# Gate and up projections of two token groups by Strassen's seven block products instead of eight

## The chip, the cores and the metric

The kernel runs on one core of one Trainium2 chip. The metric is the device time of one execution in microseconds (us); the time of a kernel is the median of its runs. Its engines are called PE (TensorE, the matrix multiplier), DVE (VectorE), ACT (ScalarE), POOL (GpSimd) and SP (SyncE, which here issues the DMAs). They run beside each other, each through its own instructions in order, and wait for each other by semaphores. PE reads a stationary and a moving matrix from SBUF and adds into PSUM, which has eight banks of 128 x 512 fp32 here.

## The reference

Four blocks follow each other on 2 x 1024 tokens of width 512, each with a layernorm in front and a residual behind; only the last sum is returned:

```python
x = x + attn_a(layernorm(x))   # gated linear attention, 4 heads of 128, chunks of 128 tokens
x = x + ffn(layernorm(x))
x = x + attn_b(layernorm(x))   # softmax attention over 1024 tokens
x = x + ffn(layernorm(x))      # the same weights again

def _qlinear(x, wq, scale):
    W = (wq.astype(float32) - 128.0) * scale[:, None]
    return einsum('bsd,hd->bsh', x, W)
def ffn(x):
    gate = silu(_qlinear(x, wq_gate, s_gate))    # 512 -> 1408
    up = _qlinear(x, wq_up, s_up)                # 512 -> 1408
    return _qlinear(gate * up, wq_down, s_down)  # 1408 -> 512
```

The codes of the FFN weights are integers from 0 to 63, so a weight without its scale is a small integer. All else is fp32.

## The kernel before

*Numbers.* PE multiplies in fp32r, which keeps fewer bits than fp32. `split` (L74) makes two fp32r parts of an fp32 tile: ACT casts (L76), DVE or POOL subtracts (L77). A product of two split matrices takes three matmuls (`mm3`, L93), a product with an FFN weight two, since the integer weight needs no second part.

*Stages.* The 2048 tokens are 16 tiles of 128 (`NT`), or 4 groups of 512 (`NST`). In order: attention a with a prologue that also multiplies the two pairs of weights of attention b together (`weight_product`: M at the start, V in the last two chunks); `ffn` on x1 ("f"); attention b; `ffn` on x3 ("g"). x1, x2 and x3 lie in DRAM between stages.

*Attention a* is a loop over 16 chunks t. In it stand in program order: a head of q for a later group (`q_head`), k and v of the next chunk (`kv_tile`), its decay matrix (`decay`, with a row loaded by SP and masked on POOL, L358), and `scores`, in which k is turned (pkT, L418) and the state updated (pd, L427). `k_norm` of the next chunk is called there: squares on ACT, sums on DVE, a power on POOL (L400), then kb on DVE (L403) and kw on POOL (L410). kb feeds the next pkT, kw the next pd. Layernorms of later groups are spread over the chunks by the list `ln_at`.

*Layernorm of a group* is `ln_step` (L170): four steps, one a tile, on DVE with one power on POOL (L114) and a 32 x 32 transposition on DVE (L178); with the fourth, 16 DMAs on SP's queue (L187) finish the transposition; a fifth step splits the result into xh and xl.

*An FFN* first loads the codes and takes 128 off them on POOL (L91; 22 loads of 128 x 512 for gate and up, 11 for down). Then for each group of 512 tokens: for each of `KH` = 11 blocks j of 128 hidden units, 8 matmuls for gate and 8 for up (L551, L552), Silu on ACT (L555), the product with up on DVE (L558), and its split into hh and hl. When all 11 blocks are done, the four token tiles get their down product, 22 matmuls each (L578, L579), the scale on DVE (L580), the residual on POOL (L582) and the store. The layernorm steps of the next group are called in the j loop; in the last group the steps that the caller gave (`after`).

*Attention b* has, for each batch, q, v, then a loop over 8 query tiles: scores, softmax, transposition of the probabilities through DRAM (stored by L662, loaded as ptl by four DMAs, L670, and split into pth and ptl), and the context pob (L685 calls `mm3`), whose sum x3 is stored. In the second batch the layernorm of g's first group is called in this loop, as the first four and the seventh step.

*Order.* The program is written as above, and a scheduler fixes each engine's order at build time by a model of its own of the times; `issue_after` holds some work behind named instructions. Buffers come from pools with a number of copies: an instruction that writes a new copy waits for the last reader of the oldest. SP issues DMAs in its order, and a DMA that waits holds those behind it.

## Time and profile before

| what | value |
|---|---|
| median of 3 runs | 1009.73 us (1009.11 to 1016.08) |
| profiled execution, its own time | 1013.86 us |
| its span, from the first to the last record | 1012.0 us |
| mean granted PE clock in it | 0.993 of full speed |
| PE busy | 987.8 us, 98% |
| DVE, ACT, POOL busy | 531.3, 294.7, 195.8 us |
| gate and up matmuls (L551, L552) | 4 groups of 352 records, 137.0 to 137.7 us by their durations |
| down matmuls (L578, L579) | 726 records, 275.4 us by their durations |
| code passes on POOL (L91) | 66, 0.65 to 0.76 us each |

The table says how long each engine was busy, not what set the end. A matmul's duration overlaps with the next one's, so that the sum of the durations is larger than the time they took; the steps between starts tell that. In a group of instructions the parts are: line, engine, operation, output <- inputs, shapes and count; after the bar the busy time in us and the mean in ns; after the second bar the idle time of that engine in front of them and whose end it waited for. In a timeline a line begins with the start and the duration in us.

### The profile page before, as it was taken

How to read it: one execution, taken by the hardware profiler on the slowest of the kernel's cores; microseconds unless marked ns; L12 is line 12 of the kernel's file. 1: busy time of each engine (PE TensorE's matmuls, PEld its weight loads, DVE VectorE, ACT ScalarE, POOL GpSimd, SP SyncE). 2: the span in 40 equal slices, each digit the busy share in tenths (PEclk: the TensorE clock that was granted, in tenths of full speed). 3: DMA queues.
4: the chain of work that ended last, by engine and by line, in shares of the span. 5: the costliest groups of instructions: out<-in, count | busy, mean ns of one | idle time of the engine just before them, and what ended most of it. 6: DMA issues, size and time to landing. Idle time of an engine off the chain costs nothing.

```text
span 1012.0 us, 12887 instructions
## 1 busy us (share of the span) xinstructions
PE 987.8 (98%) x4618; PEld 818.6 (81%) x4618; DVE 531.3 (53%) x1075; ACT 294.7 (29%) x554; POOL 195.8 (19%) x242
## 2 busy tenths in 40 slices
PE   9999999988989999999999999999979999999998
PEld 7888888877778888888888887888857888888887
DVE  7577666895574635273634445644536623233232
ACT  5642333331332413232222223222213413122130
POOL 5333222555312020112200000021002020100201
PEclk9999999999999999999999999999998999999999
DMA  8625251479746150454425378477677250110201
GB/s 293 222 86 140 71 118 63 144 189 279 247 111 146 27 136 26 84 206 118 155 42 115 86 165 170 89 177 182 162 146 180 39 125 2 42 42 1 84 1 62
DMA packets 249854, 120.71 MB, mean 119 GB/s; under 512 B 191232, under 2 KB 207936, under 8 KB 249792
## 3 DMA queue, kind: packets, MB, share of 16 engines
q1 hardware_dynamic: 249792, 119.91, 45.6%
q8 instruction: 36, 0.59, 0.2%
q14 instruction: 26, 0.21, 0.1%
HBM read 75.79 MB, written 29.39 MB: 104 GB/s over the span
## 4 chain that ended last, share of the span: by engine, by line
PE 79%; DMA 9%; SPq 5%; DVE 3%; issue 1%; ACT 1%; POOL 1%; ACTq 0%; DVEq 0%; POOLq 0%
PE pgug L551 8%; PE pgug L552 8%; PE pguf L551 6%; PE pguf L552 6%; PE pog L579 4%; PE pog L578 4%; PE pof L579 4%; PE pof L578 4%; DMA ptl<-p 3%; SPq L187 3%; DMA stg_guf<-in_wgu 2%; SPq L670 2%; DMA p<-py 2%; PE pq L96 2%; PE psc L94 1%; PE psc L96 1%
## 5 line engine op out<-in xcount | busy, mean ns | idle before, releaser
L551 PE MATMUL pguf<-xh_f,wguf 128*128 128x512 f32 x352 | 137.5, 391 | 0.3 <-ACT sgf L555 0.3
L551 PE MATMUL pgug<-xh_g,wgug 128*128 128x512 f32 x352 | 137.7, 391 | 0.0
L552 PE MATMUL pgug<-xl_g,wgug 128*128 128x512 f32 x352 | 137.6, 391 | 0.0
L552 PE MATMUL pguf<-xl_f,wguf 128*128 128x512 f32 x352 | 137.0, 389 | 0.0
L551 PEld LDWEIGHTS pguf<-xh_f,wguf 128*128 128x128 f32 x352 | 66.2, 188 | 14.8 <-issue 1.1
L551 PEld LDWEIGHTS pgug<-xh_g,wgug 128*128 128x128 f32 x352 | 66.6, 189 | 13.9
L552 PEld LDWEIGHTS pgug<-xl_g,wgug 128*128 128x128 f32 x352 | 66.5, 189 | 14.0
L552 PEld LDWEIGHTS pguf<-xl_f,wguf 128*128 128x128 f32 x352 | 66.2, 188 | 13.7
L578 PE MATMUL pof<-wdf,hhf 128*128 128x512 f32 x176 | 68.9, 395 | 2.5 <-ACT hhf L76 2.5
L578 PE MATMUL pog<-wdg,hhg 128*128 128x512 f32 (+1 forms) x187 | 68.9, 377 | 0.0
L579 PE MATMUL pog<-wdg,hlg 128*128 128x512 f32 (+1 forms) x187 | 68.8, 377 | 0.0
L579 PE MATMUL pof<-wdf,hlf 128*128 128x512 f32 x176 | 68.8, 395 | 0.0
L558 DVE SCALAR_TENSOR_TENSOR sgg<-pgug,cols,sgg 128x512 f32<-128x512 f32 x44 | 32.9, 748 | 58.0 <-PE pgug L552 58.0
L94 PE MATMUL pob<-vh,pth 128*128 128x512 f32 x128 | 50.7, 396 | 10.6 <-ACT pth L76 10.6
L114 POOL TENSOR_TENSOR rs_g<-ve_g,mhalf 128x1 f32<-128x1 f32 x16 | 8.9, 561 | 247.8 <-DVE ve_g L112 247.8
L582 POOL TENSOR_TENSOR xrg<-og,xrg 128x512 f32<-128x512 f32 x15 | 19.3, 1288 | 187.8 <-DVE og L580 169.6
L76 ACT CAST hhf<-sgf 128x512 fp32r<-128x512 f32 x44 | 27.2, 621 | 84.6 <-DVE sgf L558 76.5
L555 ACT ACTIVATE sgg<-pgug,cols 128x512 f32<-128x512 f32 x44 | 30.3, 688 | 69.7 <-PE pgug L552 60.8
L94 PE MATMUL psc<-xh_b,qh 128*128 128x512 f32 x128 | 50.5, 395 | 0.0
L96 PE MATMUL psc<-xh_b,ql 128*128 128x512 f32 x128 | 50.5, 395 | 0.0
L95 PE MATMUL psc<-xl_b,qh 128*128 128x512 f32 x128 | 50.5, 394 | 0.0
L95 PE MATMUL pob<-vl,pth 128*128 128x512 f32 x128 | 50.1, 391 | 0.0
(222 smaller groups left out, 2091.6 us busy)
## 6 DMA issues: line engine op xcount, KB each, us to landing
p<-py SPq DMA_DIRECT2D x16, 512.0 KB, 3.2
ptl<-p SPq DMA_DIRECT2D x64, 128.0 KB, 3.6
stg_guf<-in_wgu SPq DMA_DIRECT2D x22, 256.0 KB, 4.3
stg_gug<-in_wgu SPq DMA_DIRECT2D x22, 256.0 KB, 3.3
xin_a<-in_x SPq DMA_DIRECT2D x16, 256.0 KB, 4.1
xra<-in_x SPq DMA_DIRECT2D x16, 256.0 KB, 2.9
row<-cl SPq DMA_DIRECT2D x16, 256.0 KB, 3.7
x<-xra SPq DMA_DIRECT2D x16, 256.0 KB, 2.1
```

The lines of the kernel that those rows point to most:

```text
L76: nc.scalar.copy(hi, src)
L94: nc.tensor.matmul(ps, lhs_hi, rhs_hi, start=first, stop=False)
L95: nc.tensor.matmul(ps, lhs_hi, rhs_lo, start=False, stop=False)
L96: nc.tensor.matmul(ps, lhs_lo, rhs_hi, start=False, stop=last)
L187: nc.sync.dma_start(out=xf[32 * b : 32 * (b + 1), :, c, :], in_=y[32 * c : 32 * (c + 1), b].rearrange("p k i q -> p (k i) q"),)
L551: nc.tensor.matmul(ps, w, xh[:, k, :], start=k == 0, stop=False)
L552: nc.tensor.matmul(ps, w, xl[:, k, :], start=False, stop=k == KD - 1)
L555: nc.scalar.activation(sg, pgu[0], AF.Silu, scale=sg_s[:, j : j + 1])
L558: nc.vector.scalar_tensor_tensor(sg, pgu[1], su_s[:, j : j + 1], sg, ALU.mult, ALU.mult)
L578: nc.tensor.matmul(ps, hh[:, cs], wd[j][:, ds], start=j == 0, stop=False)
L579: nc.tensor.matmul(ps, hl[:, cs], wd[j][:, ds], start=False, stop=j == KH - 1)
L670: nc.sync.dma_start(out=raw[32 * r : 32 * (r + 1)].rearrange("p k (c q) -> p (k c) q", c=4), in_=placed[r])
```

## The change

The gate and up weights of one hidden block are a 2 x 2 matrix of blocks (rows gate and up, columns the two halves of the 512 inputs), and the activations of two token groups are another (rows the halves, columns the groups). Their product has eight block products. The change computes it by seven, in Winograd's form of Strassen's method: four sums of weight blocks (s1 to s4), four differences of activations (T1 to T4), and seven sums of results. Each of the products still has two halves of 128 inputs and two fp32r parts of the moving side, 4 matmuls of 512 columns.

- *Weights.* `combine_weights` and `down_weights` are called in chunks 1 to 11 of attention a: codes are loaded, 128 taken off, the four sums made on POOL, and all stored to DRAM. In the FFN, `stationary` loads the seven matrices of a block, 0.92 MB in two DMAs, for each block of each pair of groups, and `wd` is loaded ready made.
- *Activations.* `combine` gives 12 steps: differences in place (on POOL for f's first pair, else DVE), and the split of seven results. f's first pair is combined in chunks 12 to 15, g's in the last tiles of attention b, the second pair of each in the down loop of the first.
- *Results.* In PSUM: X starts with P1, Y with P6, Z with P5, V with P7; ACT copies X and Z, DVE adds; then, one block later (`finish`), P2, P3 and P4 are added by PE on top of what DVE wrote to Z and V.
- *Hidden activations.* They are kept in fp32 (`ha`, `hb`) but for tiles 0 and 1 of the pair, which are split at once (POOL subtracts, DVE for the last block); tiles 2 to 7 are split in the down loop one tile ahead, into two buffers (`hs`).
- *Pools.* The weights, the split activations and the parts share one pool of 12 slots of 128 x 2048.
- *Layernorms.* Those of groups 2 and 3 are in the j loop of the first pair; eight tiles of g are in attention b's second batch in place of four.

```diff
-    wp = ctx.enter_context(tc.tile_pool(name="weights", bufs=12))
-    sp = ctx.enter_context(tc.tile_pool(name="stage", bufs=4))
...
-    tp = ctx.enter_context(tc.tile_pool(name="xT", bufs=3))
...
+    def slot(name, dt=F32R):
+        return wp.tile([P, 2048], dt, tag="slot", name=name)
...
-    def load_codes(dst, src_ap, name):
-
-        stg = sp.tile([P, 512], I32, tag="stg", name=f"stg_{name}")
-        nc.sync.dma_start(out=stg, in_=src_ap)
-        nc.gpsimd.tensor_scalar(dst, stg, -ZERO_POINT, 1.0, ALU.add, ALU.mult)
...
+            raw = lnT[nm, st] = slot(f"xT_{nm}{st}").rearrange("p (k c) -> p k c", k=KD)
...
+            xl = lnT[nm, st]
+            xh = slot(f"xh_{nm}{st}").rearrange("p (k c) -> p k c", k=KD)
             for k in range(KD):
                 split(xh[:, k, :], xl[:, k, :], xl[:, k, :].bitcast(F32))
+            lnT[nm, st] = xh, xl
...
+    def combine(nm, pr, eng):
+        B = {}
+        def begin():
+            ra, rb = (lnT[nm, 2 * pr + n].bitcast(F32) for n in range(2))
+            B.update(B11=ra[:, 0:2], B12=rb[:, 0:2], B21=ra[:, 2:4], B22=rb[:, 2:4])
+        def part(n, src):
+            o = slot(f"{n}_{nm}{pr}").rearrange("p (s k c) -> p s k c", s=2, k=2)
+            XT[nm, pr, n] = o
+            split(o[:, 0], o[:, 1], B[src])
+        def less(dst, x, y):
+            eng.tensor_tensor(B[dst], B[x], B[y], ALU.subtract)
+        return [
+            begin,
+            lambda: part("B11", "B11"),
+            lambda: less("B11", "B12", "B11"),
+            lambda: part("T1", "B11"),
+            lambda: part("B22", "B22"),
+            lambda: less("B12", "B22", "B12"),
+            lambda: less("B22", "B22", "B11"),
+            lambda: part("T2", "B22"),
+            lambda: part("T3", "B12"),
+            lambda: part("B21", "B21"),
+            lambda: less("B21", "B21", "B22"),
+            lambda: part("T4", "B21"),
+        ]
+    def combine_weights(sp, j):
+        g, u = (sp.tile([P, 512], F32, tag="stg", name=f"{n}{j}") for n in ("cg", "cu"))
+        for n, c in enumerate((g, u)):
+            nc.sync.dma_start(out=c.bitcast(I32), in_=a["wgu"][j][:, n * 512 : (n + 1) * 512])
+            nc.gpsimd.tensor_scalar(c, c.bitcast(I32), -ZERO_POINT, 1.0, ALU.add, ALU.mult)
+        s, r = (sp.tile([P, 512], F32, tag="stg", name=f"{n}{j}") for n in ("cs", "cr"))
+        a11, a12, a21, a22 = g[:, 0:256], g[:, 256:512], u[:, 0:256], u[:, 256:512]
+        s1, s2, s3, s4 = s[:, 0:256], s[:, 256:512], r[:, 0:256], r[:, 256:512]
+        nc.gpsimd.tensor_tensor(s1, a21, a22, ALU.add)
+        nc.gpsimd.tensor_tensor(s2, s1, a11, ALU.subtract)
+        nc.gpsimd.tensor_tensor(s3, a11, a21, ALU.subtract)
+        nc.gpsimd.tensor_tensor(s4, a12, s2, ALU.subtract)
+        for n, c in enumerate((g, s, r, u)):
+            nc.sync.dma_start(out=wc_d[j][:, 2 * n : 2 * n + 2], in_=c.rearrange("p (n c) -> p n c", n=2))
+    def down_weights(sp, j):
+        c = sp.tile([P, 512], F32, tag="stg", name=f"cd{j}")
+        nc.sync.dma_start(out=c.bitcast(I32), in_=a["wd"][j])
+        nc.gpsimd.tensor_scalar(c, c.bitcast(I32), -ZERO_POINT, 1.0, ALU.add, ALU.mult)
+        nc.sync.dma_start(out=wd_d[j], in_=c)
+    def stationary(j, name):
+        w = slot(f"wc{name}_{j}").rearrange("p (n c) -> p n c", n=8)
+        nc.sync.dma_start(out=w[:, 0:6].bitcast(F32), in_=wc_d[j][:, 0:6])
+        nc.sync.dma_start(out=w[:, 6:7].bitcast(F32), in_=wc_d[j][:, 7:8])
+        return w
+    def products(ps, w, nm, pr, n, first):
+        m, x = {
+            "P1": (0, "B11"), "P2": (1, "B21"), "P3": (5, "B22"), "P4": (6, "T4"),
+            "P5": (2, "T1"), "P6": (3, "T2"), "P7": (4, "T3"),
+        }[n]
+        o = XT[nm, pr, x]
+        for k in range(2):
+            for s in range(2):
+                nc.tensor.matmul(
+                    ps,
+                    w[:, m, k * P : (k + 1) * P],
+                    o[:, s, k, :],
+                    start=first and k == 0 and s == 0,
+                    stop=k == 1 and s == 1,
+                    skip_group_check=n != "P6",
+                )
...
-            (x1, "f", 0, (8, 9, 10, 11, 14)),
+            (x1, "f", 0, (8, 8, 9, 9)),
+            (x1, "f", 1, (10, 10, 11, 11)),
         ):
             for i, t in enumerate(its):
                 ln_at.setdefault(t, []).append((src, nm, g, i))
+        moving = combine("f", 0, nc.gpsimd)
+        wcs = []
...
+            if 1 <= t <= KH:
+                combine_weights(sp, t - 1)
+                down_weights(sp, t - 1)
+            if t >= NT - 4:
+                for _ in range(3):
+                    moving.pop(0)()
+            if t == NT - 1:
+                wcs += [stationary(j, "f0") for j in range(2)]
...
+            fh = fctx.enter_context(tc.tile_pool(name=f"ffnh{nm}", bufs=1))
+            f1 = fctx.enter_context(tc.tile_pool(name=f"ffn1{nm}", bufs=2))
+            fw = fctx.enter_context(tc.tile_pool(name=f"ffnw{nm}", bufs=KH))
+            fp = fctx.enter_context(tc.tile_pool(name=f"ffn{nm}", bufs=4))
+            wd = []
+            for pr in range(2):
+                if pr == 0:
+                    early = [lambda g=g, i=i: ln_step(src, nm, g, i) for g in (2, 3) for i in range(ST)]
+                    late = combine(nm, 1, nc.vector)
...
+                ha = fh.tile([P, 2, KH, P], F32, tag="ha", name=f"ha{nm}{pr}")
+                hb = fh.tile([P, ST, KH, P], F32, tag="hb", name=f"hb{nm}{pr}")
+                hs = {}
...
+                def h_split(i, js, src, eng):
+                    if i not in hs:
+                        hs[i] = f1.tile([P, 2, KH, P], F32R, tag="hs", name=f"hs{nm}{pr}_{i}")
+                    split(hs[i][:, 0, js], hs[i][:, 1, js], src, eng)
+                def finish(j, w, X, Z, V, up):
+                    products(X, w, nm, pr, "P2", False)
+                    products(Z, w, nm, pr, "P3", False)
+                    products(V, w, nm, pr, "P4", False)
+                    tiles = lambda x: x.rearrange("p (i c) -> p i c", c=P)
+                    su = su_s[:, j : j + 1]
+                    sg = fp.tile([P, 512], F32, tag="sg", name=f"sg{nm}{pr}_{j}")
+                    nc.scalar.activation(sg, X, AF.Silu, scale=sg_s[:, j : j + 1])
+                    nc.scalar.activation(hb[:, :, j], tiles(Z), AF.Silu, scale=sg_s[:, j : j + 1])
+                    h01 = sg[:, 0:256]
+                    nc.vector.scalar_tensor_tensor(h01, V[:, 0:256], su, h01, ALU.mult, ALU.mult)
+                    nc.vector.scalar_tensor_tensor(
+                        ha[:, :, j], tiles(V[:, 256:512]), su, tiles(sg[:, 256:512]), ALU.mult, ALU.mult
+                    )
+                    nc.vector.scalar_tensor_tensor(hb[:, :, j], tiles(up), su, hb[:, :, j], ALU.mult, ALU.mult)
+                    for i in range(2):
+                        h_split(i, j, h01[:, i * P : (i + 1) * P], None if j == KH - 1 else nc.gpsimd)
...
-                    for s in range(2):
-                        ps = psum(f"pgu{nm}{st}_{j}_{s}")
-                        for k in range(KD):
-                            w = wgu[j][:, s * 512 + k * P : s * 512 + (k + 1) * P]
-                            nc.tensor.matmul(ps, w, xh[:, k, :], start=k == 0, stop=False)
-                            nc.tensor.matmul(ps, w, xl[:, k, :], start=False, stop=k == KD - 1)
-                        pgu.append(ps)
-                    sg = fp.tile([P, 512], F32, tag="sg", name=f"sg{nm}{st}_{j}")
-                    nc.scalar.activation(sg, pgu[0], AF.Silu, scale=sg_s[:, j : j + 1])
-                    hh = f1.tile([P, 512], F32R, tag="hh", name=f"hh{nm}{st}_{j}")
-                    hl = f1.tile([P, 512], F32R, tag="hl", name=f"hl{nm}{st}_{j}")
-                    nc.vector.scalar_tensor_tensor(sg, pgu[1], su_s[:, j : j + 1], sg, ALU.mult, ALU.mult)
-                    split(hh, hl, sg)
-                    hT.append((hh, hl))
-                    if steps and (len(steps) > 1 or j == KH - 1):
-                        ln_step(*steps.pop(0))
-                for i in range(ST):
-                    for step in steps:
-                        ln_step(*step)
-                    steps = []
-                    t = st * ST + i
-                    cs = bass.ts(i, P)
+                    for n in range(len(wcs), min(j + 3, KH)):
+                        wcs.append(stationary(n, f"{nm}{pr}"))
+                    w = wcs[j]
+                    X, Y, Z, V = (psum(f"p{n}{nm}{pr}_{j}") for n in "XYZV")
+                    for ps, n in ((X, "P1"), (Y, "P6"), (Z, "P5"), (V, "P7")):
+                        products(ps, w, nm, pr, n, True)
+                    u2 = fp.tile([P, 512], F32, tag="sg", name=f"u2{nm}{pr}_{j}")
+                    nc.scalar.copy(u2, X)
+                    nc.vector.tensor_tensor(u2, Y, u2, ALU.add)
+                    up = fp.tile([P, 512], F32, tag="sg", name=f"up{nm}{pr}_{j}")
+                    nc.scalar.copy(up, Z)
+                    nc.vector.tensor_tensor(Z, Z, u2, ALU.add)
+                    nc.vector.tensor_tensor(V, V, u2, ALU.add)
+                    nc.vector.tensor_tensor(up, V, up, ALU.add)
+                    if begun:
+                        finish(*begun)
+                    begun = j, w, X, Z, V, up
+                    if early:
+                        early.pop(0)()
+                    if pr == 0:
+                        d = fw.tile([P, 512], F32R, tag="wd", name=f"wd{nm}{j}")
+                        nc.sync.dma_start(out=d.bitcast(F32), in_=wd_d[j])
+                        wd.append(d)
...
+                finish(*begun)
+                wcs = []
+                for i in range(2 * ST):
+                    t = pr * 2 * ST + i
+                    if 1 <= i < 2 * ST - 1:
+                        n = i + 1
+                        for js in (slice(0, 6), slice(6, KH)):
+                            h_split(n, js, ha[:, n - 2, js] if n < ST else hb[:, n - ST, js], None)
...
-                            hh, hl = hT[j]
-                            nc.tensor.matmul(ps, hh[:, cs], wd[j][:, ds], start=j == 0, stop=False)
-                            nc.tensor.matmul(ps, hl[:, cs], wd[j][:, ds], start=False, stop=j == KH - 1)
+                            nc.tensor.matmul(ps, hs[i][:, 0, j], wd[j][:, ds], start=j == 0, stop=False)
+                            nc.tensor.matmul(ps, hs[i][:, 1, j], wd[j][:, ds], start=False, stop=j == KH - 1)
...
+                    for _ in range(2):
+                        if late:
+                            late.pop(0)()
+                    if pr == 0 and i == 4:
+                        wcs = [stationary(n, f"{nm}1") for n in range(2)]
+    b_first = [lambda g=g, i=i: ln_step(x2, "b", g, i) for g in range(2) for i in range(ST)]
+    b_split = [lambda g=g: ln_step(x2, "b", g, ST) for g in range(2)]
+    ffn(x1, x2, "f", wcs, (b_first, b_split))
...
-                nxt = (x2, "b", 2 * b + 2) if b + 1 < NB else (x3, "g", 0)
-                if i < 4:
-                    ln_step(*nxt, i)
-                if i == 6:
-                    ln_step(*nxt, 4)
-                    if b + 1 < NB:
+                if b + 1 < NB:
+                    if i < 4:
+                        ln_step(x2, "b", 2 * b + 2, i)
+                    else:
+                        ln_step(x2, "b", 2 * b + 3, i - 4)
+                    if i == 6:
+                        ln_step(x2, "b", 2 * b + 2, 4)
                         xTs[b + 1, 0] = lnT["b", 2 * b + 2]
-                if b + 1 < NB and i >= 4:
-                    ln_step(x2, "b", 2 * b + 3, i - 4)
+                else:
+                    if i < 6:
+                        for n in (0, 1) if i < 2 else (0,):
+                            g = 2 * i + n if i < 2 else i + 2
+                            ln_step(x3, "g", *divmod(g, ST))
+                    else:
+                        for _ in range(5):
+                            moving.pop(0)()
...
+        for _ in range(2):
+            moving.pop(0)()
+        wcs = [stationary(n, "g0") for n in range(2)]
```

## The prediction

> **What bounds the kernel now.** I read the table of engines first, then the chain that ended last, the windows by stage, the list of PE's waits, and the timelines around the places that change.
>
> ```profile
> span 1012.0 us, 12887 instructions
> PE 987.8 (98%) x4618; PEld 818.6 (81%) x4618; DVE 531.3 (53%) x1075; ACT 294.7 (29%) x554; POOL 195.8 (19%) x242
> PE 79%; DMA 9%; SPq 5%; DVE 3%; issue 1%; ACT 1%; POOL 1%; ACTq 0%; DVEq 0%; POOLq 0%
> ```
>
> TensorE is busy for all but 24.2 of 1012.0 us, so removed matmuls are worth their full time, and every new hole in PE costs its full length. What a matmul is worth is its pitch, since their ends overlap:
>
> ```profile
> 399.81 0.39 PE L551 MATMUL pguf<-xh_f,wguf 128*128 128x512 f32 x1
> ...
> 401.63 0.39 PE L551 MATMUL pguf<-xh_f,wguf 128*128 128x512 f32 x1
> ```
>
> Eight steps lie between these starts: 1.82 / 8 = 0.2275 us each, not the 0.39 in the column of durations. The windows (PE, PEld, DVE, ACT, POOL busy; clock; DMA share; GB/s) show where there is room:
>
> ```profile
> 100.00:200.00 100.00, 100.00 (x594) 86.94 (x593) 69.62 (x171) 37.17 (x81) 32.82 (x36) 1.00 0.36 101
> 200.00:225.00 25.00, 21.57 (x138) 18.48 (x137) 23.08 (x51) 8.93 (x20) 13.77 (x17) 1.00 0.70 174
> 225.00:250.00 25.00, 22.40 (x117) 19.45 (x116) 15.91 (x36) 3.96 (x6) 13.45 (x21) 0.93 0.93 269
> 800.00:950.00 150.00, 150.00 (x663) 124.22 (x662) 49.23 (x71) 35.35 (x55) 14.87 (x12) 1.00 0.16 46
> ```
>
> In attention a PE never waits while POOL is a third busy; its end (200 to 250) is where PE idles, 3.4 and 2.6 us; in the FFN (800 to 950) everything but PE is below 35%.
>
> **The change part by part,** against the profiled execution (1013.86 us: the span and 1.86 around it), which is 4.1 above the median of 1009.73.
>
> 1. *Matmuls.* Per hidden block and pair of groups 7 products of 4 replace 8 of 4. There are 11 x 2 x 2 = 44 such blocks: 44 x 4 = 176 fewer, and the built instruction order has 4362 matmul rows before, 4186 after. 176 x 0.2275 = **-40.0**. Everything below is what this pays for.
>
> 2. *Sums of weights in attention a.* Chunks 1 to 11 each get, on POOL, 3 code passes of 128x512 (0.69 by the row of L91) and 4 sums of 128x256. No row has such a sum; bounds: rs of one column, 0.55, and kw of 512, 1.04. I take 0.65, by the code pass of twice the width at 0.69. Per chunk 3 x 0.69 + 4 x 0.65 = 4.7 us; 11 chunks 51 us. On SP 3 loads and 5 stores, 8 issues of 0.33 to 0.4, so 2.9 us a chunk. In a settled chunk the cover is this:
>
> ```profile
> 103.93 1.01 POOL L400 TENSOR_TENSOR s<-ss,mhalf 128x4 f32<-128x4 f32 x1 [0.22 <-DVE ss L398]
> 105.71 0.69 DVE L403 TENSOR_TENSOR kb<-sWk,s 128x512 f32<-128x512 f32 x1
> 106.62 1.04 POOL L410 TENSOR_TENSOR kw<-sWk,s 128x512 f32<-128x512 f32 x1 [1.67 <-DVE s L408]
> 113.35 0.60 PE L418 MATMUL pkT<-ident,kb 128*128 128x128 f32 x4
> ```
>
> kb is done 7 us before its transpose, kw some 6 us before pd. A POOL sum that waits for its codes (a 256 KB code load lands in 4.3) holds s, kw, sdec, rs and the mask (L358) behind it. Load, passes and store by stage slots of four make a round of 4.3 + 4.7 + about 2.5 for a store (x1's lands in 2.1, issue 0.35) = 11.5 us against a chunk of 13, so it keeps up, later. At the start it does not: s(0) is at 41.7 and s(1) at 55.3, and two rounds stand between them in program order: 41.7 + 1.0 + 2 x 11.5 = 66, kb(1) at 67, wanted by pkT(1) at 62.2. That is 5 us of stall, 2 more for kw: 7, and 1 for later slips: **+8**, bounds 0 (the scheduler finds room) to 22 (two more such slips).
>
> 3. *End of attention a.* Four differences 128x1024 on POOL (twice kw's 1.04 to L582's 1.29: 2.1 to 2.6 each, some 10 in all) and the four casts and subtractions of 1024 on DVE (py's 1.24) come among the last chunks; the chain of code loads and passes that made the 3.4 and 2.6 us holes goes. Late next are kb(15) behind DVE's 1024-wide work (5 us) and the V product. **0**, bounds -6 to +8.
>
> 4. *The gate/up loop.* A block is 28 x 0.2275 = 6.4 us. DVE gets 4 combining passes and 3 products (four and one of 512 at 0.60 pitch, two of 256 at 0.43): 3.9; ACT two copies, two Silu, two casts of 128 : 0.6 + 0.6 + 1.4 + 0.8 = 3.4. Both are below 6.4. Two of the additions write PSUM in place, which no row shows; between the price of a row that reads PSUM (0.68) and double it, DVE comes to 3.9 to 5.1, still below 6.4, so 0 at both ends; without that cover each us above 6.4 would cost 44. Weights stream at 0.92 MB per 6.4 us, 144 GB/s; the window 0 to 25 us moved 292. But the same queue carries the layernorm's transposing DMAs:
>
> ```profile
> 72.97 10.80 SPq L187 DMA_DIRECT2D xl_a<-y_a  x16
> ```
>
> They stand ahead of the weight loads of blocks 6 and 10, in every pair with such layernorms (f0, f1, g0). A load is called three blocks ahead, but of twelve slots seven hold activations, and a load's slot comes free only as an older block ends, so I count a lead of 64 matmuls, 14.6 us, against 10.8 + 0.35 + about 6 to land (stg_df: 5.8) = 17: 2.5 late, in three pairs at one block or at both, 7.5 to 15; some of it earlier loads absorb. I take **+6**, bounds 0 to 18.
>
> 5. *From gate/up to down.* Before, PE crossed with one wait, 2.5 us for hh in front of pof. Now tiles 2 to 7 are split only in the down loop into two buffers: tile 2 waits until tile 0's last matmul. At the entry the last block's chain is bare: Silu 0.69, product 0.43, cast 0.39, subtraction 0.34, part of it twice, about 2, less some that tile 0's first ten blocks cover (22 matmuls run in order of blocks, 5.0 us a tile): 1.5. A later tile's split, casts and subtractions of 768 and 640, is a chain of about 2.6 and fits behind one tile of 5.0; where DVE's combining (two steps of 1.24 a tile, in f's and g's first pair) stands between, tile 2 is some 2.5 later. Four entries: 4 + 4 + 1.5 + 1.5 = 11, less the 2.5 that goes: **+8.5**, bounds 4 to 16.
>
> 6. *Attention b to g.* The longest wait of the profile stays, since the last context products still wait for the last pth:
>
> ```profile
> PE pob L94 <- ACT pth L76: 10.6, 4, 8.5
> ```
>
> g's 16 transposing DMAs leave this place, four weight blocks (3.7 MB, 12.7 us at 292 GB/s) come near it. **+2**, bounds 0 to 6.
>
> 7. *Clock.* After the 8.5 us hole eight matmuls started about 0.43 apart instead of 0.23:
>
> ```profile
> 762.45 0.63 PE L551 MATMUL pgug<-xh_g,wgug 128*128 128x512 f32 x1
> 762.88 0.63 PE L552 MATMUL pgug<-xl_g,wgug 128*128 128x512 f32 x1
> ```
>
> 8 x 0.2 = 1.6 us. The window 225 to 250 with 2.6 us of holes has a granted clock of 0.93. Some eight new holes: **+3**, bounds 0 to 8. The Trainium skill ("TensorE: Matmul & The Clock Gate", "Part 1: The HAM clock gate (the "warmup" mystery)") says that the clock halves only after an idle window of about 3.4 us; by it, holes of 2.5 us cost nothing more and this term is 0. The row of 0.93 speaks against it, though single holes in that window may be unseen.
>
> 8. *POOL beside DVE.* kb took 1.77 instead of 0.69 at 218.8 beside a POOL subtraction of two matrices. POOL has 51 + 10 us more of such work, nearly all off PE's path: **+1**, bounds 0 to 3. The skill ("SBUF — State Buffer", "SBUF: two separate sides") calls the port between the two an exclusive lock, held for the whole instruction, when DVE reads two SBUF operands. If each of the differences and a third of the sums met one, DVE would lose about 20 us, still hidden wherever it has slack; this speaks against putting sums on POOL near kb.
>
> Sum: -40.0 + 8 + 0 + 6 + 8.5 + 2 + 3 + 1 = **-11.5**, so 1002.4 for such an execution, and 1009.73 - 11.5 = **998** against the median.
>
> **The rivals.**
>
> *The cover holds.* POOL's rounds fit into the slack and the loads arrive: terms 2, 4, 7 and 8 fall to 3, term 5 stays at 7: -40 + 10 = -30, **980** (970 to 988). For it: POOL's 67 idle us in 100, and the stream needs half of the rate seen. Against it: program order at the start, and 10.8 us of SP in one piece.
>
> *Slower: attention a becomes paced by POOL and SP.* If landing takes 6 to 8 us under 23 MB more of traffic (the window 225 to 250 landed stg_df in 5.8 at 269 GB/s) and the stores hold the stage slots, a round is 17 us. It decides once a round passes 13 + about 2.5 of slack, 15.5; then 11 x 4 = 44, less 6 that the end gets back: 38 instead of 8. That is 998 + 30 = **1028**.
>
> *Entries and loads twice as dear.* Terms 4 and 5 at 12 and 14: 998 + 12 = **1010**, no change that shows.
>
> *It does not do what it says.* The matmuls surely go; their pitch could rise if DVE's writes into PSUM slowed them. 1232 matmuls by 0.0125 would be 15 us; nothing before shows it; inside the two last cases.
>
> **How the numbers follow.** Forecast (985 to 1010) 0.40, cover holds 0.25, paced by POOL 0.20, entries dear 0.15. Faster by over 1% means below 999.6: all of the second and rather more than half of the first, **0.48**. Slower by over 1% means above 1019.8: the third, and the tail of the fourth, **0.22**. Within 1%, which is what a measurement of this kernel can hardly tell from no change: **0.30**. All low ends of the terms together give -42 (968), all high ends +41 (1051), neither likely at once; the range takes the forecast, nearly all of the second case and the third up to its price: 975 to 1030.
>
> **What would show it.** PE instructions 4618 falling to about 4442 at a pitch of 0.2275 (step 1). Waits of PE pkT for kb and pd for kw, and PE idle from 25 to 120 us (step 2). PE idle from 200 to 250 below 6 us (3). Waits of a gate product for a DMA at blocks 6 and 10 (4). Waits of po for a split at four entries (5). The 8.5 us wait again (6). The prediction is wrong if the sums' round is not what I take, or if a slot of the pool of 12 comes free later than the count says.

## The result

The changed kernel takes 1050.42 us (median of four runs, 1049.66 to 1057.85), the kernel before 1011.12 beside it: a ratio of 1.0395, with a 95% interval of 1.0349 to 1.0441. It was forecast at 998, in a range of 975 to 1030; it is slower than the range allowed. The profiled execution took 1050.26 us, its span 1048.5, at a mean granted PE clock of 0.964 (0.993 before).

The table of engines and the chain of the changed kernel, from its page:

```profile
span 1048.5 us, 13276 instructions
PE 977.0 (93%) x4442; PEld 802.0 (76%) x4442; DVE 693.1 (66%) x1271; ACT 353.9 (34%) x686; POOL 263.9 (25%) x337
PE 54%; DVE 11%; DMA 9%; SPq 6%; issue 3%; POOL 2%; ACT 2%; ACTq 0%; DVEq 0%; POOLq 0%
```

The first two rows account for the 36.5 us by which the span grew. There are 4618 - 4442 = 176 matmuls fewer; at 0.2275 us that is -40.0, as forecast. PE's idle time went from 24.2 to 1048.5 - 977.0 = 71.5 us, **+47.3**. And PE's busy time, which should have fallen to 987.8 - 40.0 = 947.8, fell only to 977.0: **+29.2** us by which PE was longer busy than the count of its matmuls gives. -40.0 + 47.3 + 29.2 = +36.5.

The stages, in us of the span; a ends with the first gate product, f with the last down product of f, b with the first gate product of g. The holes are PE's idle times of over 0.15 us; the remainder is what matmuls and holes don't explain. Single entries hold within some 4 us: in the changed kernel twelve matmuls of attention a and six of attention b, 4.1 us, fall into f.

| stage | before | after | difference | matmuls | holes | remainder |
|---|---|---|---|---|---|---|
| attention a | 245.6 | 291.6 | +46.0 | 0 | +28.4 | +17.6 |
| FFN f | 245.6 | 237.5 | -8.0 | -20.0 | +6.0 | +6.0 |
| attention b | 271.3 | 277.6 | +6.3 | 0 | +5.6 | +0.7 |
| FFN g | 249.6 | 241.8 | -7.8 | -20.0 | +7.0 | +5.2 |

So the loss lies in attention a, where the change removes nothing. The window 50 to 200 us of the kernel before and of the changed kernel (PE, PEld, DVE, ACT, POOL busy, with the number of instructions; clock; DMA share; GB/s):

```profile
50.00:200.00 150.00, 150.00 (x877) 129.68 (x876) 106.25 (x265) 55.14 (x122) 52.22 (x60) 1.00 0.38 104
```

```profile
50.00:200.00 150.00, 134.22 (x711) 112.17 (x710) 90.83 (x208) 45.37 (x100) 87.68 (x118) 0.95 0.70 217
```

PE was never idle there and now is for 15.8 us; it gets through 711 instructions in place of 877; POOL went from a third to 58% busy, the DMA rate doubled, and the granted clock fell to 0.95. POOL is far from full, so that its throughput alone is unlikely to be what stops PE; a run below tests it. Who holds PE up is in the list of PE's waits of the changed kernel (engine, line, tile, whom it waited for: us in total, times, longest):

```profile
PE pob L89 <- ACT pth L78: 16.2, 3, 10.0
PE pkT L510 <- DVE s L500: 5.9, 2, 3.2
PE pd L519 <- POOL kw L502: 5.3, 6, 1.5
PE pS L534 <- ACT kT L512: 4.9, 2, 2.9
PE pV L89 <- ACT V L78: 4.8, 1, 4.8
PE pog L714 <- DVE hsg L79: 4.3, 3, 2.1
PE pof L714 <- DVE hsf L79: 4.0, 3, 1.8
...
PE pkT L510 <- DVE kb L495: 3.0, 2, 1.6
...
PE pXf L276 <- DMA wcf<-wc: 1.7, 2, 1.4
```

pkT, pd and pS, all in the loop over chunks, wait for 5.9 + 5.3 + 4.9 + 3.0 = 19.1 us; before, the first two waited for 2.0 and 1.4. Not all of it comes from the sums: in the run without them, below, these waits are still 5.6. One such place, from the timeline of the changed kernel (start, duration, engine, line, what; in brackets the idle time before it and what ended that):

```profile
139.36 0.49 SPq L243 DMA_DIRECT2D cg<-in_wgu  x1
...
141.51 0.15 DVE L490 TENSOR_SCALAR ss<-ss 128x4 f32<-128x4 f32 x1
...
144.04 0.62 POOL L244 TENSOR_SCALAR cg<-cg 128x512 f32<-128x512 int32 x1 [3.40 <-issue]
...
144.62 1.04 POOL L525 TENSOR_TENSOR sdec<-state,ec 128x512 f32<-128x512 f32 x1
...
145.63 0.62 POOL L244 TENSOR_SCALAR cu<-cu 128x512 f32<-128x512 int32 x1
...
146.21 1.01 POOL L492 TENSOR_TENSOR s<-ss,mhalf 128x4 f32<-128x4 f32 x1
...
147.26 0.68 DVE L493 TENSOR_TENSOR s<-s,beta 128x4 f32<-128x4 f32 x1 [3.85 <-POOL s L492]
...
147.98 1.17 DVE L495 TENSOR_TENSOR kb<-sWk,s 128x512 f32<-128x512 f32 x1
...
149.30 0.63 PE L510 MATMUL pkT<-ident,kb 128*128 128x128 f32 x4 [1.61 <-DVE kb L495]
...
150.99 1.83 PE L519 MATMUL pd<-sWv,kw 128*128 128x128 f32 x8 [1.07 <-POOL kw L502]
```

s, the power for the next kb, has its input at 141.66. POOL stands idle for 3.40 us in front of the pass on cg, whose codes were called for at 139.36; then come that pass, sdec and the pass on cu, and s starts at 146.21, 4.55 late. DVE waits 3.85 for it, PE 1.61 for kb and 1.07 for kw. At this place the profile names no releaser for POOL's idle time ("issue"); over all chunks it mostly names the code loads, as the groups of the three code passes show (count; busy us, mean ns; idle time in front, and what ended it):

```profile
L244 POOL TENSOR_SCALAR cg<-cg 128x512 f32<-128x512 int32 x11 | 7.3, 661 | 8.7 <-DMA cg<-in_wgu 4.0 <-issue 3.4 <-POOL kw L502 0.6
L244 POOL TENSOR_SCALAR cu<-cu 128x512 f32<-128x512 int32 x11 | 7.3, 661 | 4.7 <-DMA cu<-in_wgu 2.5 <-DVE z L357 1.8 <-issue 0.4
L258 POOL TENSOR_SCALAR cd<-cd 128x512 f32<-128x512 int32 x11 | 7.3, 659 | 19.8 <-DMA cd<-in_wd 15.8 <-DVE ve_a L105 3.0 <-POOL s L492 1.0
```

That is 33.2 us in which POOL stood in front of work whose result is first read in the FFN, 22.3 of them put down to a code load. In the chunk shown, work that PE needed in the same chunk stood behind it in the queue.

Each such hole is paid twice. PE's timeline of the changed kernel after a hole of 2.33 us:

```profile
109.02 0.43 PE L336 MATMUL pab<-xh_a,wab 128*48 128x512 f32 x1 [2.33 <-ACT xh_a L78]
...
109.99 0.39 PE L91 MATMUL pWk<-Wk,xl_a 128*128 128x512 f32 x1
110.22 0.52 PE L89 MATMUL pWk<-Wk,xh_a 128*128 128x512 f32 x1
110.53 0.63 PE L90 MATMUL pWk<-Wk,xh_a 128*128 128x512 f32 x1
110.96 0.63 PE L91 MATMUL pWk<-Wk,xl_a 128*128 128x512 f32 x1
111.39 0.63 PE L89 MATMUL pWk<-Wk,xh_a 128*128 128x512 f32 x1
...
113.86 0.39 PE L89 MATMUL pWv<-Wv,xh_a 128*128 128x512 f32 x1
```

Some 1.2 us after PE resumed, the starts are 0.43 apart in place of 0.23, for 3.4 us, which loses 1.7. By the traces' records of the granted clock, the changed kernel has 14 stretches of low clock that lose 1.7, 3.4 or 5.1 us each, 37.5 together; 30.2 of them fall on time in which PE works, the rest lies in its holes and costs nothing. The kernel before had 3 that lost 6.8, of which 5.2 fell on work; a fourth began after its last matmul. The difference, 25.0, is most of the 29.2 of PE's busy time. The other 4.2 are of the size that comes from counting: the holes cut PE's work into 45 pieces in place of 15, and the last matmul of each counts with its duration of 0.39 instead of its step of 0.23.

### The profile page after: what moved, and what is told of

Read it like the earlier page. It is cut to its first block, busy times and chain, and to the rows that moved or that the text cites. A ratio compares the mean times of both kernels' runs of the same rounds, so it can differ in the third digit from the quotient of the medians.

```text
span 1048.5 us, 13276 instructions
## 1 busy us (share of the span) xinstructions
PE 977.0 (93%) x4442; PEld 802.0 (76%) x4442; DVE 693.1 (66%) x1271; ACT 353.9 (34%) x686; POOL 263.9 (25%) x337
## 3 DMA queue, kind: packets, MB, share of 16 engines
q1 hardware_dynamic: 268800, 171.82, 57.8%
## 4 chain that ended last, share of the span: by engine, by line
PE 54%; DVE 11%; DMA 9%; SPq 6%; issue 3%; POOL 2%; ACT 2%; ACTq 0%; DVEq 0%; POOLq 0%
SPq L185 4%; PE pog L714 4%; PE pof L714 4%; PE pof L713 3%; PE pog L713 3%; PE pXg L276 3%; PE pXf L276 3%; DMA p<-py 3%; PE pVg L276 3%; PE pZg L276 3%; PE pZf L276 3%; PE pVf L276 3%; DMA ptl<-p 3%; PE pYf L276 2%; PE pYg L276 2%
## 5 line engine op out<-in xcount | busy, mean ns | idle before, releaser
L714 PE MATMUL pog<-wdg,hsg 128*128 128x512 f32 (+1 forms) x187 | 70.5, 387 | 4.3 <-DVE hsg L79 4.3
L714 PE MATMUL pof<-wdf,hsf 128*128 128x512 f32 x176 | 69.2, 398 | 4.0 <-DVE hsf L79 4.0
L713 PE MATMUL pog<-wdg,hsg 128*128 128x512 f32 (+1 forms) x187 | 70.5, 386 | 2.4 <-ACT hsg L78 2.4
L713 PE MATMUL pof<-wdf,hsf 128*128 128x512 f32 x176 | 69.4, 399 | 3.1 <-ACT hsf L78 3.1
L89 PE MATMUL pob<-vh,pth 128*128 128x512 f32 x128 | 51.7, 404 | 16.2 <-ACT pth L78 16.2
L91 PE MATMUL pob<-vh,ptl 128*128 128x512 f32 x128 | 50.9, 397 | 0.0
L90 PE MATMUL psc<-xT_b,qh 128*128 128x512 f32 x128 | 50.5, 394 | 0.0
L276 PE MATMUL pXg<-B_g,wcg 128*128 128x512 f32 x176 | 48.0, 395 | 0.4 <-DMA wcg<-wc 0.4
L276 PE MATMUL pXf<-B_f,wcf 128*128 128x512 f32 x176 | 46.4, 391 | 1.7 <-DMA wcf<-wc 1.7
L276 PE MATMUL pVg<-T_g,wcg 128*128 128x512 f32 x176 | 46.9, 389 | 0.0
L276 PE MATMUL pVf<-T_f,wcf 128*128 128x512 f32 x176 | 46.9, 389 | 0.0
L714 PEld LDWEIGHTS pog<-wdg,hsg 128*128 128x128 f32 x187 | 36.0, 193 | 11.9 <-DVE hsg L79 5.2
L713 PEld LDWEIGHTS pog<-wdg,hsg 128*128 128x128 f32 x187 | 36.1, 193 | 10.3 <-ACT hsg L78 3.7
L714 PEld LDWEIGHTS pof<-wdf,hsf 128*128 128x128 f32 x176 | 33.7, 192 | 12.2 <-DVE hsf L79 5.2
```

The lines of the kernel that those rows point to most:

```text
L89: nc.tensor.matmul(ps, lhs_hi, rhs_hi, start=first, stop=False)
L90: nc.tensor.matmul(ps, lhs_hi, rhs_lo, start=False, stop=False)
L91: nc.tensor.matmul(ps, lhs_lo, rhs_hi, start=False, stop=last)
L276: nc.tensor.matmul(ps, w[:, m, k * P : (k + 1) * P], o[:, s, k, :], start=first and k == 0 and s == 0, stop=k == 1 and s == 1, skip_group_ ...
L713: nc.tensor.matmul(ps, hs[i][:, 0, j], wd[j][:, ds], start=j == 0, stop=False)
L714: nc.tensor.matmul(ps, hs[i][:, 1, j], wd[j][:, ds], start=False, stop=j == KH - 1)
```

## The experiments

My theory was that attention a is held up because POOL's passes are tied to DMAs: POOL, in order, waits for codes and for stage slots with the chunk's own work behind it. The rivals were POOL's load by itself, the DMAs' load by themselves, and the combining of activations at the stage's end. "First gate product" is the end of attention a in the profile, 245.6 before and 291.6 after. In some runs a few matmuls of attention a come after it; where that matters, the text says so.

### The DMAs of the sums without the passes

```diff
-            nc.gpsimd.tensor_scalar(c, c.bitcast(I32), -ZERO_POINT, 1.0, ALU.add, ALU.mult)
-        s, r = (sp.tile([P, 512], F32, tag="stg", name=f"{n}{j}") for n in ("cs", "cr"))
...
-        for n, c in enumerate((g, s, r, u)):
+        for n, c in enumerate((g, g, u, u)):
```

> The sums' DMAs alone: per block the code loads and the same number and size of stores as in the changed kernel, without any pass on POOL (the two code tiles are stored twice; the output is not the reference's). If the traffic and SP's issues cause the loss, attention a stays at 280 us or more. If it is POOL, by its time or by its standing behind code loads, attention a is as without the sums, within 5 us.

Measured: 1036.3 us, ratio 1.0241 (1.0207 to 1.0274); first gate product at 268.9, far from the 280 by which the traffic would have been the main cause.

### The sums behind the next chunk's kb

The calls of `combine_weights` and `down_weights` move by one level into the block that holds work until the next chunk's kb:

```diff
                 for ins in normed.get(t + 1, ()):
                     late.enter_context(tc.issue_after(ins))
...
-            if 1 <= t <= KH:
-                combine_weights(sp, t - 1)
-                down_weights(sp, t - 1)
+                if 1 <= t <= KH:
+                    combine_weights(sp, t - 1)
+                    down_weights(sp, t - 1)
```

> The whole change, but the sums of a chunk are held behind the next chunk's kb, as the layernorm steps are, so that they stand behind s and kw instead of in front. If the place in POOL's order is what costs, attention a falls by 15 us or more, and so does the total (1035 or less). If POOL's time, or the traffic, costs wherever it stands, it falls by less than 8 us.

Measured: 1048.43 us, ratio 1.0361 (1.0315 to 1.0406); first gate product at 289.6, 2.0 earlier. The hold only shifts the round by a part of a chunk: behind one kb it stands in front of the next chunk's s. POOL and PE in the timeline of this run, at the place that was shown of the change:

```profile
143.60 0.62 POOL L244 TENSOR_SCALAR cg<-cg 128x512 f32<-128x512 int32 x1 [2.89 <-issue]
...
145.95 1.02 POOL L492 TENSOR_TENSOR s<-ss,mhalf 128x4 f32<-128x4 f32 x1
...
149.04 0.63 PE L510 MATMUL pkT<-ident,kb 128*128 128x128 f32 x4 [1.37 <-DVE kb L495]
```

The order is the same, and so is the wait. The run tells against this cure by program order, with which 15 us or more were expected; it doesn't take the waits away, and so leaves open whether they are the cause.

### No sums at all

The FFNs load as many bytes in as many DMAs as in the changed kernel, but from another matrix in DRAM.

```diff
+        m = m_d[j % KD].rearrange("p (n c) -> p n c", n=4)
-        nc.sync.dma_start(out=w[:, 0:6].bitcast(F32), in_=wc_d[j][:, 0:6])
-        nc.sync.dma_start(out=w[:, 6:7].bitcast(F32), in_=wc_d[j][:, 7:8])
+        nc.sync.dma_start(out=w[:, 0:4].bitcast(F32), in_=m)
+        nc.sync.dma_start(out=w[:, 4:7].bitcast(F32), in_=m[:, 0:3])
...
-            if 1 <= t <= KH:
-                combine_weights(sp, t - 1)
-                down_weights(sp, t - 1)
...
```

> No sums of weights and no passes on down codes in attention a: no code load, no POOL pass, no store. The FFN loads as many bytes in as many DMAs from another matrix in DRAM, so the output is not the reference's. Attention a (start to the first gate product of f) lasted 245.6 us before, 291.6 with the change, 268.9 with the sums' DMAs alone. If those DMAs cost something by their traffic, attention a falls well below 268.9, to 246 to 255. If they cost nothing and the other 23 us are the rest of what moved into attention a (combining f's first pair there, the second group's layernorm, the shared pool), it stays at 263 to 270. Total 1010 to 1022 by the first, 1030 to 1037 by the second.

Measured: 1020.04 us, ratio 1.0084 (1.0041 to 1.0126), first gate product at 261.8. The window 50 to 200 without sums, columns as above:

```profile
50.00:200.00 150.00, 150.00 (x869) 129.44 (x869) 104.94 (x268) 51.99 (x115) 47.75 (x57) 1.00 0.40 103
```

PE is whole again, at full clock. The sums cost 1050.42 - 1020.04 = 30 us, the largest part of the loss. But without them the change still gains nothing: it is 8 us slower than the kernel before, with 40 us of matmuls gone.

### The passes without the DMAs

The passes read a constant tile into the stage slots; nothing is loaded or stored. The FFNs' loads are as in the run without sums.

```diff
-            nc.gpsimd.tensor_scalar(c, c.bitcast(I32), -ZERO_POINT, 1.0, ALU.add, ALU.mult)
+            nc.gpsimd.tensor_scalar(c, sd_b.bitcast(I32), -ZERO_POINT, 1.0, ALU.add, ALU.mult)
...
-        for n, c in enumerate((g, s, r, u)):
-            nc.sync.dma_start(out=wc_d[j][:, 2 * n : 2 * n + 2], in_=c.rearrange("p (n c) -> p n c", n=2))
```

> The sums' POOL work alone: the same three passes and four sums a block, on a constant in SBUF and the stage buffers, without code loads and stores (the FFN loads from another matrix, the output is not the reference's). If POOL's time as such is what pushes s and kw back, attention a lasts what it lasts without the sums plus some 20 us. If only POOL's standing behind code loads does, it is within 5 us of that without the sums.

Measured: 1028.29 us, ratio 1.0141 (1.0112 to 1.0171); first gate product at 268.5. The window:

```profile
50.00:200.00 150.00, 147.35 (x828) 126.20 (x827) 112.76 (x260) 51.49 (x114) 94.39 (x123) 0.99 0.40 102
```

POOL is busier here than in the changed kernel (94.4 against 87.7 us), and PE loses 2.65 us in place of 15.8. The load on POOL by itself costs 6.7 to 8.3 us, so it is not the main cause of the 30.

### Both, but not tied to each other

The same loads and stores and as many passes of the same shapes; but the passes read a constant and write a bf16 scratch tile, so POOL never waits for a DMA, nor a DMA for POOL.

```diff
-            nc.gpsimd.tensor_scalar(c, c.bitcast(I32), -ZERO_POINT, 1.0, ALU.add, ALU.mult)
+            nc.gpsimd.tensor_scalar(scratch, sd_b.bitcast(I32), -ZERO_POINT, 1.0, ALU.add, ALU.mult)
+        a11, a12 = sd_b[:, 0:256], sd_b[:, 256:512]
+        for _ in range(4):
+            nc.gpsimd.tensor_tensor(scratch[:, 0:256], a11, a12, ALU.subtract)
...
-        for n, c in enumerate((g, s, r, u)):
+        for n, c in enumerate((g, g, u, u)):
```

> The sums' DMAs and the sums' POOL work in the same kernel, but not tied to each other: the codes are loaded and stored back as they are (3 loads, 5 stores a block), and POOL makes its three passes and four sums on a constant into a scratch tile of bf16, so that POOL waits for no load and no store waits for POOL (the output is not the reference's). Attention a lasted 261.8 us without sums, 268.9 with the DMAs alone, 268.5 with the passes alone, 291.6 with both tied together. If POOL's waiting for the loads with s, kw and the mask queued behind it is what makes the whole larger than its parts, attention a is 261.8 + 7.1 + 6.7 = 276 here, at most 279. If the two only get in each other's way by being there at the same time, it stays at 286 or more.

Measured: 1034.29 us, ratio 1.0235 (1.0187 to 1.0283); first gate product at 276.3. The window:

```profile
50.00:200.00 150.00, 141.85 (x786) 119.91 (x785) 101.33 (x243) 50.80 (x114) 84.31 (x107) 0.97 0.77 236
```

The DMA rate is higher than in the changed kernel (236 against 217 GB/s), POOL as busy (84.3 against 87.7), and PE loses half as much, 8.15 against 15.8. The five runs stand together so:

| sums | median, us | over no sums | first gate product | over no sums |
|---|---|---|---|---|
| none | 1020.0 | | 261.8 | |
| passes alone | 1028.3 | +8.3 | 268.5 | +6.7 |
| DMAs alone | 1036.3 | +16.3 | 268.9 | +7.1 |
| both, untied | 1034.3 | +14.3 | 276.3 | +14.5 |
| both, tied (the change) | 1050.4 | +30.4 | 291.6 | +29.8 |

By either column the tie costs 15 to 16 us over both loads untied, half of what the sums cost. How the other half divides is not settled: by the first gate product, passes and DMAs add up to the untied run, by the median they don't. With the DMAs alone 28 matmuls of attention a stand behind the first gate product, with the other four 12, so that 3.6 us of the delay show up only in f. Each kernel is scheduled anew, too, and the medians of the three runs in the middle are of two executions, so that single microseconds in this table are not to be read as one cause's.

By the profiled executions, 5.0 of the 15.3 us that the tie costs in attention a are idle PE (35.7 against 30.7) and 10.5 are low clock while PE works (20.4 against 9.9): tied, the holes cut PE's work there into 26 pieces, untied into 19.

The untied run takes the tie away at both ends. In the changed kernel SP stands too, in front of stores that wait for POOL's passes, with later loads behind them (from its list of SP's waits):

```profile
SPq L253 <- POOL cg L244: 15.5, 8, 3.1
...
SPq L259 <- POOL cd L258: 12.9, 8, 3.7
```

No run removes only one of the two waits, POOL's for loads or SP's for POOL, so how the 15 us divide between them is open.

### The differences of f's first pair left out

As the run without sums, and the four subtractions on POOL in front of f's first pair are left out.

```diff
         def less(dst, x, y):
+            if nm == "f" and pr == 0:
+                return
             eng.tensor_tensor(B[dst], B[x], B[y], ALU.subtract)
```

> As without the sums, and the four differences of f's first pair on POOL are left out too (the splits stay; the output is not the reference's). If the differences and their lock against DVE hold kb and the V product at the end of attention a, it is shorter by 5 us or more than without the sums alone; if the splits on ACT and DVE and the late loads of V's weights do, by less than 3.

Measured: 1019.26 us, ratio 1.0057 (1.0035 to 1.0079); first gate product at 260.6 against 261.8. The four differences take 9.8 us of POOL (2.41 to 2.48 each) and cost about 1 in the median. In attention a it is more: without sums twelve of its matmuls, 2.7 us, stand behind the first gate product, here none, so that it is some 4 us shorter, between the two bounds.

### The first weights of g behind the last probabilities

In the changed kernel's SP queue, between attention b and g:

```profile
784.47 0.38 SPq L264 DMA_DIRECT2D wcg<-wc  x1
...
788.22 0.44 SPq L265 DMA_DIRECT2D wcg<-wc  x1
...
790.55 0.38 SPq L805 DMA_DIRECT2D p<-py  x1
...
799.29 2.35 SPq L813 DMA_DIRECT2D ptl<-p  x4
```

Eight weight loads were issued just before the last probabilities are stored (790.55). That store lands 8.7 us after its issue, and the loads back are issued then; before the change it landed after 3.5, and the loads back followed after 4.1 (750.43 to 754.54). PE waits 10.0 us in one piece for pth. The experiment holds these weight loads:

```diff
     def stationary(j, name):
+        with tc.issue_after(held["ptl"]) if name == "g0" else nullcontext():
+            return stationary_now(j, name)
...
-                nc.sync.dma_start(
+                held["ptl"] = nc.sync.dma_start(
```

> The whole change; only the loads of g's first weights are held behind the last loads of ptl in attention b, instead of standing before the last store of p. In the changed kernel the store of the last p was issued 6 us after the first of these loads, its ptl loads 8.7 us later (4.1 before), and PE waited 10.0 us for pth. If the 3.7 MB in front of the store are the cause, that wait falls by 3 to 5 us and the total by 2 to 5 (g's first product may then wait for its weights). If the chain through DRAM is what ends last anyway, nothing moves (within 1.5).

Measured: 1042.35 us, ratio 1.028 (1.025 to 1.031), 8 us less than the change. PE's wait for pth in it:

```profile
PE pob L89 <- ACT pth L78: 9.6, 3, 6.7
```

That is 6.6 us less than 16.2, and 3.3 less in the longest piece; the total fell by more than the 2 to 5 expected. The store lands after 3.3 us. From the first matmul of attention b to the end the profile is 9.4 us shorter, since low clock went with the holes: between 780 and 815 us it loses 3.4 in place of 8.5, of which 1.7 in place of 5.0 fall on work. So here a store and reload that PE waits for was held up by the prefetch issued just before it.

### The sums in f instead of attention a

If the loss comes from where the sums are made, they belong where POOL has no consumer on PE's path. f's first two groups are computed by eight products as before, from codes that are loaded for them anyway; the sums are made from these tiles in their gate and up loop and stored for the three other pairs; the hold of the previous run is kept. Of the 176 matmuls 132 are saved, -30.0 us.

```diff
-            if 1 <= t <= KH:
-                combine_weights(sp, t - 1)
-                down_weights(sp, t - 1)
...
+                    if st == 0 and j >= 5:
+                        combine_weights(sp, j - 5, wgu[j - 5])
+                    if st == 1 and j < 5:
+                        combine_weights(sp, j + 6, wgu[j + 6])
```

> The whole computation, rearranged: f's first pair of groups is computed with eight products as before the change, and the sums of weights are made during it on POOL from the codes that lie in SBUF anyway and stored; seven products from f's second pair on, so 132 instead of 176 matmuls fewer (-30.0 us). Attention a has no sums, no combining and one group's layernorm less, as before the change; g's first weights are held behind the last ptl loads. If the loss in attention a is all from what the change put there, attention a is 246 to 252 us and the total 990 to 1002: -30.0, entries of three pairs some +7 and their clock +5, attention b +3. If the shared pool of slots or the order at the start costs (pkT of the first chunk was at 57.3 without the sums against 50.9), attention a stays at 256 or more and the total at 1002 to 1012.

Measured: 1015.41 us, ratio 1.0041 (1.0007 to 1.0075); first gate product at 256.1. Its waits at the end of attention a:

```profile
PE pguf L653 <- POOL wgu L243: 4.8, 1, 4.8
...
PE pV L90 <- POOL V L79: 2.6, 1, 2.6
```

Attention a is still 10.5 us longer than before, though it holds neither sums nor combining. The total lies above the 1002 to 1012 that were expected for this case. What is left in attention a of the change are its pools: the one of 12 slots of 128 x 2048, and a stage pool that ends with attention a. The first pkT is at 57.8 (50.9 before, 59.4 after), and f waits 4.8 for its codes, a wait that the change itself doesn't have.

### The same with the pools of the kernel before

Weights again in 12 tiles of 1024, the split activations in their pool of three, the stage pool open from the start; g's second combining waits for the split of tile 2.

```diff
-    wp = ctx.enter_context(tc.tile_pool(name="slots", bufs=12))
+    wp = ctx.enter_context(tc.tile_pool(name="weights", bufs=12))
...
+    tp = ctx.enter_context(tc.tile_pool(name="xT", bufs=3))
...
+    sp = early_pools.enter_context(tc.tile_pool(name="stage", bufs=4))
...
+                        with tc.issue_after(held["hs", 2]):
+                            for _ in range(2):
+                                if late:
+                                    late.pop(0)()
```

> The whole computation, as in the run with f's first pair by eight products, but with the pools of the kernel before (12 buffers of 1024 for weights, three of each half of the activations) in place of the 12 slots of 2048: the parts and the streamed weights lie in pairs of weight buffers or in activation buffers. Attention a and f's first pair are then built as before the change. Besides, the combining of g's second pair is held behind the split of the third tile at the entry to its down loop. With the slots attention a lasted 256.1 us (245.6 before), the first chunk's pkT came at 57.8 (50.9), and the first gate product waited 4.8 us for its codes. If the slots were the cause of these, attention a is 245 to 248 us, and the total is 990 to 1002 with the 132 matmuls (-30.0) showing. If the order of the work is the cause whatever the pools, attention a stays at 254 or more and the total at 1006 or more. If three pairs of buffers for the streamed weights are too few, gate products wait for them for more than 10 us in all.

Measured: 1011.15 us against 1015.02 of the kernel before beside it, ratio 0.9958 (0.9933 to 0.9984). The first pkT is back at 51.4 and the first gate product at 242.1, so the 10.5 us were the pools' doing (slots, stage and the order that follows from them; which of them, these runs don't tell). Attention a came back as expected, the total of 990 to 1002 did not. Two large waits are left, one in attention b and one at the start of f (from 264.35 to 270.58 us), where a gate product waits for a Silu:

```profile
PE pob L96 <- ACT pth L78: 15.2, 3, 10.6
PE pguf L655 <- ACT sg8f L659: 6.2, 1, 6.2
```

### And the combining for g behind the last exponentials

The steps of `combine` for g's first pair are held until the last exponentials of attention b are issued.

```diff
-                nc.scalar.activation(
+                held["pe"] = nc.scalar.activation(
...
-                        for _ in range(5):
-                            moving.pop(0)()
+                        with tc.issue_after(held["pe"]):
+                            for _ in range(5):
+                                moving.pop(0)()
...
-        for _ in range(2):
-            moving.pop(0)()
+        with tc.issue_after(held["pe"]):
+            for _ in range(2):
+                moving.pop(0)()
```

> The rearranged kernel with the pools of before, and one edit: the combining of g's first pair in attention b is held behind the exponentials of the last query tile. Without the hold, DVE and ACT made differences and splits of 128x1024 between the last maximum and the exponential (the second step of the maximum at 751.66 us where the scores had ended at about 746), and PE waited 10.6 us for the last pth. If those passes in front of the softmax are what made the wait longer than the 8.5 us before the change, it falls to 5 to 8.5 us, attention b gets 3 to 7 us shorter, and the ratio to the kernel before goes from 0.996 to 0.989 to 0.993. If the combining then stands in front of g's first products instead, or the chain through DRAM sets the wait, the total moves by less than 2 us.

Measured: 1003.54 us against 1013.72, ratio 0.9905 (0.9873 to 0.9938): 1% faster than the kernel before, a small gain, with an interval wholly below 1. From its page and its list of waits:

```profile
span 997.9 us, 13212 instructions
PE 962.2 (96%) x4486; PEld 793.5 (80%) x4486; DVE 648.6 (65%) x1225; ACT 338.4 (34%) x653; POOL 246.0 (25%) x313
```

```profile
PE pob L96 <- ACT pth L78: 9.5, 4, 6.9
PE pguf L655 <- ACT sg8f L659: 6.0, 1, 6.0
PE pog L778 <- DVE hsg L79: 5.2, 4, 1.9
```

Of the 30.0 us of matmuls 14.1 remain in the span (1012.0 to 997.9; this execution was the fastest of its four) and 10.2 in the medians. Attention a ends at 244.6, within 1 us of the kernel before. The wait for pth is 5.7 shorter than in the run above. What the span gives back is idle PE, 35.7 us against 24.2, and 962.2 - (987.8 - 30.0) = 4.4 us by which PE is longer busy than its matmuls' count gives: -30.0 + 11.5 + 4.4 = -14.1.

## Why the prediction was wrong, step by step

*What bounds the kernel:* right, PE's holes cost their full length, and more: they also cost clock.

*1, matmuls, -40.0:* right in count and pitch. The fear that PSUM written by DVE would raise the pitch did not come true.

*2, sums in attention a, +8 (0 to 22):* **this step failed**; the sums cost 30, in attention a 16.5 of idle PE and 11.8 of low clock (35.7 against 19.2, and 20.4 against 8.6 without sums). The passes were sized well (51 us of POOL forecast; the groups of the changed kernel, 661, 659, 736, 788, 732 and 789 ns, 11 times each with the pass on cg and cu twice, come to 55). What failed is the argument of cover: a round of load, passes and store of 11.5 us was set against a chunk of 13, as if it ran beside the chunk. It runs in POOL's queue. POOL waits inside the round, and s, kw and sdec wait with it, and the round takes longer: the codes of one block were called 14.8 us after those of the block before, in the mean (37.9 to 186.3 in ten steps), and a chunk took 15.4 from pkT to pkT (59.4 to 213.1 in ten steps) in place of 12.5 without sums (57.3 to 182.7) and 13.6 untied (61.9 to 197.8). Round and chunk run at one pace; in the chunk shown, s starts 3.1 us ahead of its pkT (146.21 to 149.30), where it was 9.4 in the settled chunk of the kernel before (103.93 to 113.35). The text named that s, kw and the mask are held behind a sum that waits, and priced it only for the first chunk. The rival "paced by POOL and SP" had the right place and sign; it was priced at 38 for the stage in place of 8, and set to decide only from a round of 15.5 us. Moving the sums behind kb gave 2 us, untying them 15 to 16.

*3, end of attention a, 0 (-6 to +8):* without sums the first gate product is 16.2 later than before, 18.9 with the twelve matmuls of attention a that stand behind it there. With the run with the sums in f at 256.1, combining and the layernorms in front of it have 8.4 of that, or 13.2 if the 4.8 us for codes are taken off; the differences on POOL are some 4 of it. This is the upper bound or above it. **No step had** the other 5.7 to 10.5, the pools of the change, gone when the old pools were put back. The prediction read the pools only for the lead of the weight loads in the FFN.

*4, gate/up loop, +6 (0 to 18):* too dear. The loop's waits for its weights (pXf for wc) are 1.7 us in f and 0.4 in g. The additions in PSUM took 690 to 697 ns, the low end of the bound.

*5, entries, 11 less 2.5 = +8.5 (4 to 16):* right in mechanism; the four entries have holes of 4.84, 2.30, 5.14 and 1.52 us, 13.8 less 2.5 = 11.3, and a stretch at low clock behind two of them. DVE's split of T stands in front of the split that the down product waits for, from the timeline of the changed kernel:

```profile
379.10 1.92 DVE L79 TENSOR_TENSOR T_f<-xT_f,T_f 128x1024 fp32r<-128x1024 f32 x1
...
383.01 0.79 PE L714 MATMUL pof<-wdf,hsf 128*128 128x512 f32 x1 [1.84 <-DVE hsf L79]
```

*6, b to g, +2 (0 to 6):* +6.3 in attention b, and the weight blocks that were named as coming near hold up the store; holding them back took 8 us off the total, clock included.

*7, clock, +3 (0 to 8):* **failed, by as much as the second**: +25 on matmuls, of which 19 in attention a; 11.8 of these are in the 30 of the second step, too. It was counted from one hole of 8.5 us at 1.6, and eight holes. There were 14 stretches, half of them after holes or pairs of holes of 2 to 3.2 us. The four executions had granted clocks of 0.958 to 0.971, so this term is not the same in each. The rule of the Trainium skill that was weighed there ("TensorE: Matmul & The Clock Gate", "Part 1: The HAM clock gate (the "warmup" mystery)"), by which holes of 2.5 us cost nothing, was the further off: the rows after 109.02 show a hole of 2.33 that cost 1.7 in clock.

*8, POOL beside DVE, +1:* kb took 1.17 in place of 0.69 at 147.98. The runs don't price the term by itself. With the passes alone, DVE was busy 112.76 us with 260 instructions in the window, without sums 104.94 with 268, so DVE's work takes longer beside POOL's passes; what that has of the 6.7 to 8.3 us of that run is open.

Outside the two failed steps and the pools the sum came near: f and g gave 15.8 in place of the 40.0 - 14.5 = 25.5 of steps 1, 4 and 5. Of the missing 9.7, 4.1 are the eighteen matmuls of attention a and b that fall into f, and about 3 are low clock; the holes, 13.0, stayed below the 14.5. Attention a, forecast at +8 and part of the 3 of clock, took 46.0.

## What to carry to other kernels

Work that is put on an engine's queue "in its idle time" is cheap only if it never waits. If it hangs on a DMA, everything behind it on that engine hangs on the DMA too: here 55 us of passes on an engine that was two thirds idle cost 30 us, 8 without DMAs and about 14 with as many DMAs but no tie. Put such work where nothing behind it on that queue is needed soon; hold a prefetch until the transfer that PE waits for is issued; and leave the pools of a stage that the change doesn't need alone. Price a new hole in PE at its length and, from about 2 us on, at some 1.7 us more for the clock in most cases.
